# A perceiver kernel with two attention stages around 64 experts: a longer second chain in the first stage, a norm on another engine, and scores at another place in the second stage

## The chip, the cores and the metric

The kernel runs on one core of a Trainium2 chip. The metric is the device time of one execution, in microseconds (us); for the kernel before it is 2828.25 us, the median of three runs (2827.0 to 2829.42). A core has a matrix engine (TensorE, "PE" in the profile, with its weight loads as "PEld"), a vector engine (VectorE, "DVE"), an activation engine (ScalarE, "ACT"), a general engine (GpSimd, "POOL") and a queue of transfers that is fed by SyncE ("SP"). Each engine works through its own instructions in order, and the engines wait for each other by semaphores.

## The reference, cut to what matters

All data is float32. There are 64 sequences of 32 tokens, width 256 (2048 tokens in all), and 64 contexts of 257 rows of width 256, one for each sequence. Two layers follow each other; every step is added to the token stream x.

- Layer 0, cross attention: tokens are layer-normed twice, context rows once (with gain g and offset b); keys and values come from the context rows and the sequence's own tokens; 16 heads of 64; queries and keys are divided by their root mean square; softmax over 289 positions with a mask.
- Layer 0, self attention over the 32 tokens of a sequence, 16 heads of 16, with normed queries and keys.
- Layer 0, mixture of experts: a gate takes 8 of 64 experts for each token, an expert holding 128 tokens at most; every expert is a gated product 256 to 128 to 256. A shared gated product (512 wide) is added with a sigmoid gate.
- Layer 1, cross attention to the same contexts (257 rows), then a self attention with latent projections and a rotation of the positions, then a feed-forward of three 256x256 products in a row and a tanh.

The steps that the change touches most are, for a context of layer 0, the norm and the attention:

```
xn = (x - mean(x)) / sqrt(var(x) + eps) * g + b
k, v = split([xn, ln] @ Wkv)
attn = softmax(where(mask, rmsnorm(q) @ rmsnorm(k).T * scale, -max))
out = (attn @ v) @ Wout + bout
```

with mean and variance over a row's 256 values and ln the sequence's own normed tokens. All other steps are left as they are by the change.

## The kernel before, in words

The 2048 tokens are 16 tiles t of 128 tokens; tile t holds sequences s = 4t to 4t + 3, and b is the place of s in its tile. x stays on the chip for the whole run. PSUM, where products land, is cut into 8 banks (`bank`), which are given out in turn. TensorE's instructions run in the order in which the program is written; the other engines' orders come from a scheduler that follows modelled times. Most work is written as Python generators; each `yield` is a place where the other chain's work can be put in between.

**Stage 1** (`before`, L372). The first chain, of class CrossFirst, goes over the contexts s:
- `load` brings the context rows (cx, 2 x 128 x 256).
- `prepare` (L1156) norms them: statistics and two TENSOR_SCALAR on VectorE (`layernorm`, L140), then gain and offset by two instructions on GpSimd (L1160, L1161).
- `turn` transposes them (L1173) and copies them to xT (L1176, ScalarE; the sequence's own tokens by L1177).
- `keys` makes the keys in eight column blocks (32 matmul instructions of 289 columns, L167 psA<-xT,wk), copied to kT by L1201 and L1203 in turn, and squares them to `sq` (L1206).
- `norms` sums the squares over a head (L1218), `spread` spreads them over the rows (L1239), `scores` makes the scores (L1258) and the softmax (L1267, L182, L184, L197).
- `weigh` transposes the weights (L207) and copies them to `at` (L208); `values` multiplies `at` with cx (L221) and then with the value weights, with a copy to yT (L231, L233).

`queries(t)` (L1090) prepares a tile's queries: the two norms, transposes, the product with wq and more transposes. In the loop (L467) the pieces of several contexts are interleaved: keys, norms, spread and scores of s + 2, turn of s + 3, prepare of s + 4, load of s + 5, weigh and values of s. The second chain, `tail` (L516), takes a finished tile through the output product and the addition to x (`heads_out`, L237), the first self attention (`self_first`, L527: `normed`, product to qk, L552 transposes, L573 scores, softmax over heads, `attend_self` with the transposed weights eT of L297 and the products of L310), and the gate (`route`: L614, L617 and the writing of the tokens to their experts' rows, L645). It is resumed by `slot()`, each call of which takes every running chain one `yield` further. There are three slots for each s and two in the last s of a tile, so 11 for each tile; a tile's tail takes 14 resumptions, and tile 14's has an extra pause of HOLD resumptions.

**Stage 2** (`experts`, L656). Each of 64 experts has its weights fetched 12 ahead (AHEAD), its tokens transposed and three products. At expert 12 `after_weights` (L795) loads the weights of stage 3 and makes two derived weights on TensorE: the latent weights, and the feed-forward's three matrices joined to one (`ffn_weights`, from f_a, L167 psA<-f_a,f_a1T and psA<-mid,f_wT). The shared product's pieces are spread between the experts.

**Stage 3** (`after`, L808). For each s: scores of s + 2 (L167 psY<-xT,qk, softmax L1357 and L1358), a slot, `weigh` of s (transposes L1375, copies to `at` L1376), a slot, `values` of s (L167 psA<-at,cx, L1388). The chain in the slots is `follow`: output product, second self attention (`self_second`, with transposes L1003 and L1014, copy to qTl L1005), feed-forward. `combine` gathers the experts' rows of a tile (L780) and adds them to x (L791).

Two flags differ between the stages: `slack`, off in stage 1 and on in stage 3, adds one pause behind a norm and one in `attend_self`.

Of the kernel before, what the change touches and what calls it, by code (L numbers as in the profile page):

```python
# [14 lines left out]
ALU = mybir.AluOpType  # L15
# [69 lines left out]


def done(steps):
    for _ in steps:
        pass


class Kernel:
# [58 lines left out]

    def normed(self, t):

        z = self.wk.tile([P, 1, D], F32, name="z")
        self.layernorm(z, self.x[:, t : t + 1, :])
        yield
        if self.slack:
            yield
        zT = self.wk.tile([P, 2, P], F32, name="zT")
        self.transposed(zT, z[:, 0, :])  # L160
        yield
        return z, zT
# [5 lines left out]

    def add_to_x(self, t, ps, bias=None):
        nc, xt = self.nc, self.x[:, t, :]  # L170
        if bias is not None:
            nc.gpsimd.tensor_tensor(xt, xt, bias, ALU.add)
        nc.vector.tensor_tensor(xt, xt, ps, ALU.add)
# [62 lines left out]

    def heads_out(self, t, yT, wv, wo, bias, split=False):  # L237


        nc = self.nc  # L240
        oT = self.wkh.tile([P, 8, P], F32, name="oT", tag="q", bufs=1)
        for half in range(2):
            ps = self.bank("psY")
            for p in range(4):
                for odd in range(2):
                    h = 2 * (4 * half + p) + odd
                    at = h // 4 * 4 + PLACES[h // 4 % 2].index(h % 4) if split else h
                    self.product(
                        ps[DH * odd : DH * odd + DH, p * P : (p + 1) * P],
                        [wv[:, k, h * DH : (h + 1) * DH] for k in range(2)],  # L250
                        [yT[:, k, at, :] for k in range(2)],
                    )
            nc.any.tensor_copy(
                oT[:, 4 * half : 4 * half + 4, :].rearrange("p a b -> p (a b)"), ps
            )
        yield
        ps = self.bank("psY")
        self.product(ps[:, :D], [oT[:, p, :] for p in range(8)], [wo[:, p, :] for p in range(8)])
        self.add_to_x(t, ps[:, :D], bias)

# [29 lines left out]

    def attend_self(self, t, e, recip, wo, bias):

# [4 lines left out]
        nc.vector.transpose(eT.rearrange("p a b -> p (a b)"), e.rearrange("p a b -> p (a b)"))  # L297
        yield
        if self.slack:
            yield  # L300

# [70 lines left out]
    def before(self, ctx):  # L372


        self.eb, self.vb, self.slack = 1, 2, False
        tc, nc, a = self.tc, self.nc, self.a
# [42 lines left out]
        cross.prepare(0)  # L419
        next(first)  # L420
        next(first)
        cross.prepare(1)
        for i in range(2):
            cross.load(i + 2)
            cross.turn(i)
            cross.keys(i)
            cross.norms(i)
            done(first)
            cross.spread(i)
            cross.scores(i)  # L430
        cross.load(4)
        cross.prepare(2)
        cross.prepare(3)
        cross.turn(2)

# [80 lines left out]
    def tail(self, t, yT, wv, wo, bo, sw, swo, sg, gw):  # L516

        yield from self.heads_out(t, yT, wv, wo, bo, True)
        yield
        if t == self.nt - 2:  # L520

            for _ in range(HOLD):
                yield
        yield from self.self_first(t, sw, swo, sg)
        yield from self.route(t, gw)

    def self_first(self, t, sw, swo, sg):  # L527
        nc = self.nc
        _, zT = yield from self.normed(t)
        qk = self.wk.tile([P, 2 * H, HS], F32, name="qk1", bufs=1)  # L530
# [10 lines left out]
            qk[:, :H, :], qk[:, :H, :], sg.unsqueeze(1).to_broadcast([P, H, HS]), ALU.mult  # L541
        )
        ps = self.bank("psA")
        self.product(ps[:, :D], [zT[:, k, :] for k in range(2)], [sw[:, k, 2 * D :] for k in range(2)])
# [40 lines left out]
        yield  # L585
        yield from self.attend_self(t, e, recip, swo, None)

    def route(self, t, gw):
# [29 lines left out]
        nc.vector.tensor_scalar(pr, pr, tot, None, ALU.mult)  # L618

        yield  # L620

# [34 lines left out]
    def experts(self, ctx, slot, tails):  # L656
# [94 lines left out]
        for e in range(E):  # L751
            weigh(e + AHEAD)
            fetch(e + 3)
            turn(e + 2)
            while (at - total + rest) * E < rest * e:
                next(side)
                at += 1
            inner(e + 1)
            outer(e)
            if e == AHEAD:  # L760
                self.after_weights()
        done(side)

# [33 lines left out]
    def after_weights(self):  # L797
# [7 lines left out]
        self.lat = self.latent_weights(w)  # L805
        self.ffnw = self.ffn_weights(w)

    def after(self, ctx):  # L808
        self.eb = self.vb = 1
        self.slack = True  # L810
        nc, n = self.nc, self.nb
# [25 lines left out]
        for s in range(n):  # L837
            t, b = divmod(s, NB)
            if s + 3 < n:
                cross.load(s + 3)  # L840
            if s + 2 < n:
                cross.scores(s + 2)
            if b == NB - 2 and t + 2 < self.nt:
                steps.append(cross.queries(t + 2))
                if t + 3 < self.nt:
                    steps.append(self.combine(t + 3, 3))
            slot()
            cross.weigh(s)
            slot()
            if s < 2:  # L850

                slot()
                slot()
            cross.values(s)
            if b == NB - 1:
                steps.append(self.follow(t, cross.yT, wv, wo, bo))
            slot()
# [112 lines left out]
    def self_second(self, t, wl, bl, wvo, bvo, wqk, bqk, wo, bo):  # L970
        nc = self.nc
        _, zT = yield from self.normed(t)
        lat = self.wk.tile([P, 2 * H, LAT], F32, name="lat", bufs=1)
# [42 lines left out]
        nc.any.tensor_copy(kT, ps)  # L1016
        yield


# [23 lines left out]
        yield  # L1043
        yield from self.attend_self(t, e, recip, wo, bo)

# [17 lines left out]
    def ffn(self, t, m, bias):  # L1063
        nc = self.nc
        _, zT = yield from self.normed(t)
        ps = self.bank("psA")
# [12 lines left out]
class CrossFirst:  # L1079
# [11 lines left out]
    def queries(self, t):  # L1091
# [7 lines left out]
        nc.gpsimd.tensor_tensor(ln[:, 0, :], ln[:, 0, :], self.bl, ALU.add)  # L1099
        yield  # L1100
        lnT = k.wkx.tile([P, 2, P], F32, name="lnT")
        k.transposed(lnT, ln[:, 0, :])
# [6 lines left out]
        for n in range(2):  # L1109
# [9 lines left out]
                q[:, 8 * n : 8 * n + 8, :], v, self.gam.unsqueeze(1).to_broadcast([P, 8, DH]), ALU.mult  # L1119
            )  # L1120
        nc.vector.tensor_scalar(ss, ss, float(DH) * 1e-16, None, ALU.max)
        nc.scalar.activation(ss, ss, AF.Ln)
# [33 lines left out]
    def prepare(self, s):  # L1156

        k, nc, cx = self.k, self.k.nc, self.cx[s]
        k.layernorm(cx, cx)
        nc.gpsimd.tensor_tensor(cx, cx, self.gx.unsqueeze(1).to_broadcast([P, 2, D]), ALU.mult)  # L1160
        nc.gpsimd.tensor_tensor(cx, cx, self.bx.unsqueeze(1).to_broadcast([P, 2, D]), ALU.add)  # L1161

# [123 lines left out]
class CrossSecond:  # L1286
# [7 lines left out]
    def queries(self, t):  # L1294

        k, nc = self.k, self.k.nc
        _, zT = yield from k.normed(t)
        qT = k.wk.tile([P, 8, P], F32, name="qT", bufs=1)
# [173 lines left out]
```

## Time and profile before

| | |
|---|---|
| median of three runs | 2828.25 us |
| the profiled execution | 2804.67 us |
| its span, first to last instruction | 2802.8 us |
| mean granted TensorE clock | 0.982 of full |
| moved to and from memory | 157.03 MB, mean 56 GB/s |
| costliest TensorE group, keys product (L167 psA<-xT,wk) | 517.4 us busy, 2048 instructions |
| busiest ACT group, squares (L1206) | 149.4 us, 128 instructions |
| busiest DVE groups: copies to kT (L1203), score products (L1267) | 108.4 and 102.1 us |
| POOL's gathers (L780) and writings (L645) | 131.5 and 126.5 us |

The profile is of one execution. Its page gives the busy time of each engine, the same in 40 slices of the span, the costliest groups of instructions, and the chain of work that ended last. A group's line reads: code line, engine, operation, output<-inputs, sizes, count | busy us, mean ns of one | idle time of the engine just before, and what ended most of it. The list of waits sums such idle times by what the engine waited for. Stretches are given in us from the start of the span: stage 1 runs to about 1508, the last tile's second chain to 1570, stage 2 to about 1760, stage 3 from there to the end.

### The profile page before, as it was taken

To read this page: it belongs to the slowest core of one execution; us is meant where nothing else is said; L and a number is where in the kernel's file an instruction comes from. 1 tells how busy PE (TensorE), PEld (TensorE's weight loads), DVE (VectorE), ACT (ScalarE), POOL (GpSimd) and SP (SyncE) were. 2 spreads that over 40 slices of the span, in tenths; PEclk is the share of its full clock that TensorE was granted. 3 is DMA by queue.
4 is the path that set the end of the run, shared out by engine and by line. 5 is a ranking of instruction groups with operands and counts; after the bars stand their busy time and mean duration, and the time that the engine had idled before them with its cause. 6 is when DMAs were issued, how large, how long until landed. Compare 5 with 4: busy or idle time off the path is not lost. (4 is left out here: it accounts for less than half of the span.)

```text
span 2802.8 us, 58905 instructions
## 1 busy us (share of the span) xinstructions
PE 2657.6 (95%) x23386; PEld 1824.5 (65%) x23386; DVE 1694.9 (60%) x4427; ACT 1241.6 (44%) x3436; POOL 684.3 (24%) x756
## 2 busy tenths in 40 slices
PE   6999999999999999999999799999999999999996
PEld 3556666666666666666666578667777777777764
DVE  5546666666666666666665433466666666666664
ACT  3455555555555555555554223333333333333331
POOL 5211333133313331243121200321212222121001
PEclk8999999999999999999999899999999999999997
DMA  8000011011000000000001677321211222222110
GB/s 271 16 14 18 31 33 31 18 31 33 29 18 27 26 22 18 20 19 16 18 7 38 233 237 243 91 67 54 58 51 50 59 52 58 56 51 55 33 35 5
DMA packets 136087, 157.03 MB, mean 56 GB/s; under 512 B 24024, under 2 KB 118979, under 8 KB 135812
## 3 DMA queue, kind: packets, MB, share of 16 engines
q1 hardware_dynamic: 114308, 119.65, 13.8%
q0 software_dynamic: 12288, 25.21, 3.4%
q10 hardware_dynamic: 9216, 8.39, 0.9%
q8 instruction: 185, 3.03, 0.4%
q14 instruction: 90, 0.74, 0.1%
HBM read 121.63 MB, written 37.75 MB: 57 GB/s over the span
## 5 line engine op out<-in xcount | busy, mean ns | idle before, releaser
L167 PE MATMUL psA<-xT,wk 128*128 128x289 f32 x2048 | 517.4, 411 | 7.9 <-ACT xT L1176 4.5
L167 PEld LDWEIGHTS psA<-xT,wk 128*128 128x128 f32 x2048 | 388.0, 191 | 134.8 <-issue 21.8
L780 POOL DMA_INDIRECT y<-oute,idx x128 | 131.5, 1028 | 643.4 <-DVE x L791 453.9
L167 PE MATMUL psA<-at,cx 128*128 128x512 f32 x512 | 235.4, 602 | 20.0 <-ACT qTl L1005 18.2
L221 PE MATMUL psY<-at,cx 128*128 128x512 f32 x512 | 239.8, 612 | 0.1
L167 PE MATMUL psY<-xT,qk 128*128 128x257 f32 x1024 | 234.3, 382 | 0.0
L167 PEld LDWEIGHTS psY<-xT,qk 128*128 128x128 f32 x1024 | 190.8, 190 | 35.0 <-issue 10.2
L1357 DVE TENSOR_REDUCE mx<-psY 128x1 f32<-128x257 f32 x256 | 105.7, 423 | 133.6 <-PE psY L167 133.5
L1358 ACT ACTIVATE sim<-psY,mx 128x257 f32<-128x257 f32 x256 | 121.6, 476 | 142.3 <-DVE mx L1357 142.2
L184 ACT ACTIVATE sim<-sim,mx 128x289 f32<-128x289 f32 x256 | 134.1, 526 | 100.0 <-DVE mx L182 100.0
L221 PEld LDWEIGHTS psY<-at,cx 128*128 128x128 f32 x512 | 93.5, 192 | 123.0 <-issue 108.8
L167 PEld LDWEIGHTS psA<-at,cx 128*128 128x128 f32 x512 | 92.9, 190 | 120.8 <-issue 76.7
L233 ACT COPY yT<-psY 128x512 f32<-128x512 f32 x127 | 68.2, 589 | 220.7 <-PE psY L231 220.7
L645 POOL DMA_INDIRECT buf<-z,fi x128 | 126.5, 988 | 148.0 <-DVE fi L642 102.2
L1160 POOL TENSOR_TENSOR cx<-cx,a_gx 128x512 f32<-128x512 f32 x64 | 81.8, 1278 | 292.1 <-DVE cx L140 290.3
L1206 ACT ACTIVATE sq<-kT 128x1156 f32<-128x1156 f32 x128 | 149.4, 1167 | 4.4 <-DVE kT L1203 2.8
L1201 ACT COPY kT<-psA 128x289 f32<-128x289 f32 x256 | 94.8, 389 | 104.2 <-PE psA L167 104.2
L1376 ACT COPY at<-psT 128x512 f32<-128x512 f32 x145 | 78.8, 595 | 123.4 <-PE psT L1375 118.3
L1218 PE MATMUL psB<-sq,c 128*32 128x289 f32 x1024 | 109.4, 419 | 19.7 <-ACT sq L1206 19.5
L1388 DVE SCALAR_TENSOR_TENSOR yT<-at,xT,psA 128x512 f32<-128x512 f32 x128 | 94.0, 735 | 56.1 <-PE psA L167 50.7
L167 PE MATMUL psY<-yT,wv 128*64 128x128 f32 x2048 | 121.6, 275 | 1.6 <-DVE yT L1388 1.4
L1177 POOL COPY xT<-lnT 128x64 f32<-128x64 f32 x64 | 15.3, 240 | 423.0 <-PE psA L167 299.3
(257 smaller groups left out, 5190.5 us busy)
## 6 DMA issues: line engine op xcount, KB each, us to landing
cx<-in_ctx SPq DMA_DIRECT2D x128, 256.0 KB
we<-in_m_ew SPq DMA_DIRECT2D x64, 384.0 KB
xT<-in_ctxT SPq DMA_DIRECT2D x64, 257.0 KB
buf<-zero SPq DMA_DIRECT2D x32, 256.0 KB
be<-buf SPq DMA_DIRECT2D x64, 128.0 KB
oute<-oe ACTq DMA_DIRECT2D x64, 128.0 KB
mu<-in_mask SPq DMA_DIRECT2D x16, 128.5 KB
x<-in_x SPq DMA_DIRECT2D x16, 128.0 KB
```

The lines of the kernel that those rows point to most:

```text
L167: self.nc.tensor.matmul(ps, lhsT=lhs[i], rhs=rhs[i], start=(i == 0), stop=(i == n - 1))
L184: nc.scalar.activation(sim[:, g, :], sim[:, g, :], AF.Exp, bias=mx[:, g : g + 1], accum_out=sm[:, g : g + 1])
L221: nc.tensor.matmul(ps[kc], lhsT=values[i][:, kc * P : (kc + 1) * P], rhs=at[i], start=(i == 0), stop=(i == n - 1 and tail is None),)
L645: d = nc.gpsimd.indirect_dma_start(out=self.buf[:, :], out_offset=bass.IndirectOffsetOnAxis(ap=fi[:, k : k + 1], axis=0), in_=z[:, 0, :], ...
L780: nc.gpsimd.indirect_dma_start(out=y, out_offset=None, in_=self.oute[:, :], in_offset=bass.IndirectOffsetOnAxis(ap=self.idx[:, t, k : k + ...
L1160: nc.gpsimd.tensor_tensor(cx, cx, self.gx.unsqueeze(1).to_broadcast([P, 2, D]), ALU.mult)
L1201: nc.scalar.copy(kT[:, p, :], ps[:, :JK])
L1206: nc.scalar.activation(sq[p // 4], kT[:, p - 3 : p + 1, :], AF.Square)
L1218: nc.tensor.matmul(ps[g * 32 : (g + 1) * 32, :JK], lhsT=k.pair[odd], rhs=sq[p // 4][:, p % 4, :], start=(odd == 0), stop=(odd == 1),)
L1357: nc.vector.tensor_reduce(mx[:, g : g + 1], ps[:, :J], AX.X, ALU.max, negate=True)
L1358: nc.scalar.activation(sim[:, g, :], ps[:, :J], AF.Exp, bias=mx[:, g : g + 1], accum_out=sm[:, g : g + 1])
L1388: nc.vector.scalar_tensor_tensor(self.yT[:, c, :, b * S : (b + 1) * S], self.at[:, 2, :].rearrange("p (h i) -> p h i", h=H), xT[:, c, J - ...
```

## The change

- (a) The start of stage 1 is written in another order: four resumptions of the first queries ahead of the second context's norm; loads 2, 3 and 4 together; turn and keys of context 0, the rest of the first queries, turn of 1, norms of 0, prepare of 2, spread and scores of 0, keys of 1, turn of 2, norms of 1, prepare of 3, spread and scores of 1.
- (b) The tail of stage 1 takes 26 resumptions instead of 14: a pause behind the norm, qk apart from the values, nine pauses in `attend_self`, one more in `route`. `slack` becomes an argument that counts pauses. `queries` of CrossFirst has two more yields; its product with wq is made in two halves in different slots.
- (c) In stage 1 the output product is made in two halves of 128 columns, each with its own addition of bias (GpSimd) and product (VectorE) to x.
- (d) The HOLD pause of tile 14 in stage 1 is gone; in stage 3 it stays.
- (e) The contexts' norm has its gain and offset on VectorE: four SCALAR_TENSOR_TENSOR instead of two TENSOR_SCALAR on VectorE and two TENSOR_TENSOR on GpSimd.
- (f) `ffn_weights` is called at expert 24 instead of expert 12.
- (g) In stage 3 the scores of s + 2 come behind `weigh` of s instead of ahead of the slot in front of it.
- (h) `self_second` has one more yield ahead of its score product.

```diff
+def pause(n):
+    for _ in range(n):
+        yield
...
-    def normed(self, t):
+    def normed(self, t, steps=0):
...
-        if self.slack:
-            yield
+        yield from pause(steps)
...
-    def add_to_x(self, t, ps, bias=None):
-        nc, xt = self.nc, self.x[:, t, :]
+    def add_to_x(self, t, ps, bias=None, cols=slice(0, D)):
+        nc, xt = self.nc, self.x[:, t, cols]
...
-    def heads_out(self, t, yT, wv, wo, bias, split=False):
+    def heads_out(self, t, yT, wv, wo, bias, split=False, parts=1):
...
-        yield
-        ps = self.bank("psY")
-        self.product(ps[:, :D], [oT[:, p, :] for p in range(8)], [wo[:, p, :] for p in range(8)])
-        self.add_to_x(t, ps[:, :D], bias)
+        n = D // parts
+        for i in range(parts):
+            yield
+            cols = slice(i * n, (i + 1) * n)
+            ps = self.bank("psY")
+            self.product(ps[:, :n], [oT[:, p, :] for p in range(8)], [wo[:, p, cols] for p in range(8)])
+            self.add_to_x(t, ps[:, :n], bias[:, cols], cols)
...
-    def attend_self(self, t, e, recip, wo, bias):
+    def attend_self(self, t, e, recip, wo, bias, steps):
...
-        yield
-        if self.slack:
-            yield
+        yield from pause(steps)
...
-        next(first)
-        next(first)
+        for _ in range(4):
+            next(first)
         cross.prepare(1)
-        for i in range(2):
-            cross.load(i + 2)
-            cross.turn(i)
-            cross.keys(i)
-            cross.norms(i)
-            done(first)
-            cross.spread(i)
-            cross.scores(i)
-        cross.load(4)
+        for i in range(2, 5):
+            cross.load(i)
+        cross.turn(0)
+        cross.keys(0)
+        done(first)
+        cross.turn(1)
+        cross.norms(0)
         cross.prepare(2)
+        cross.spread(0)
+        cross.scores(0)
+        cross.keys(1)
+        cross.turn(2)
+        cross.norms(1)
         cross.prepare(3)
-        cross.turn(2)
+        cross.spread(1)
+        cross.scores(1)
...
     def tail(self, t, yT, wv, wo, bo, sw, swo, sg, gw):
-        yield from self.heads_out(t, yT, wv, wo, bo, True)
-        yield
-        if t == self.nt - 2:
-            for _ in range(HOLD):
-                yield
+        yield from self.heads_out(t, yT, wv, wo, bo, True, 2)
+        yield
...
-        yield from self.attend_self(t, e, recip, swo, None)
+        yield from self.attend_self(t, e, recip, swo, None, 9)
...
             if e == AHEAD:
                 self.after_weights()
+            if e == 2 * AHEAD:
+                self.ffnw = self.ffn_weights(self.w2)
...
-            if s + 2 < n:
-                cross.scores(s + 2)
             if b == NB - 2 and t + 2 < self.nt:
...
             slot()
             cross.weigh(s)
+            if s + 2 < n:
+                cross.scores(s + 2)
             slot()
...
-        yield from self.attend_self(t, e, recip, wo, bo)
+        yield from self.attend_self(t, e, recip, wo, bo, 2)
...
     def prepare(self, s):
         k, nc, cx = self.k, self.k.nc, self.cx[s]
-        k.layernorm(cx, cx)
-        nc.gpsimd.tensor_tensor(cx, cx, self.gx.unsqueeze(1).to_broadcast([P, 2, D]), ALU.mult)
-        nc.gpsimd.tensor_tensor(cx, cx, self.bx.unsqueeze(1).to_broadcast([P, 2, D]), ALU.add)
+        mv, rs = k.stats(cx, 2)
+        for j in range(2):
+            x = cx[:, j, :]
+            nc.vector.scalar_tensor_tensor(x, x, mv[:, j, 0:1], self.gx, ALU.subtract, ALU.mult)
+            nc.vector.scalar_tensor_tensor(x, x, rs[:, j : j + 1], self.bx, ALU.mult, ALU.add)
```

More of the change, by code (lines that the diff above doesn't have):

```diff
@@ L372, in before @@
     def before(self, ctx):
-        self.eb, self.vb, self.slack = 1, 2, False
+        self.eb, self.vb = 1, 2
         tc, nc, a = self.tc, self.nc, self.a
@@ L528, in self_first @@
         nc = self.nc
-        _, zT = yield from self.normed(t)
+        _, zT = yield from self.normed(t, 1)
         qk = self.wk.tile([P, 2 * H, HS], F32, name="qk1", bufs=1)
@@ L618, in route @@
         nc.vector.tensor_scalar(pr, pr, tot, None, ALU.mult)
+        yield
         yield
@@ L805, in after_weights @@
         self.lat = self.latent_weights(w)
-        self.ffnw = self.ffn_weights(w)
     def after(self, ctx):
         self.eb = self.vb = 1
-        self.slack = True
         nc, n = self.nc, self.nb
@@ L971, in self_second @@
         nc = self.nc
-        _, zT = yield from self.normed(t)
+        _, zT = yield from self.normed(t, 1)
         lat = self.wk.tile([P, 2 * H, LAT], F32, name="lat", bufs=1)
@@ L1017, in self_second @@
         yield
+        yield
         ps = [self.bank("psB") for _ in range(4)]
@@ L1064, in ffn @@
         nc = self.nc
-        _, zT = yield from self.normed(t)
+        _, zT = yield from self.normed(t, 1)
         ps = self.bank("psA")
@@ L1100, in queries @@
         yield
+        yield
         lnT = k.wkx.tile([P, 2, P], F32, name="lnT")
@@ L1120, in queries @@
             )
+            if n == 0:
+                yield
         nc.vector.tensor_scalar(ss, ss, float(DH) * 1e-16, None, ALU.max)
@@ L1296, in queries @@
         k, nc = self.k, self.k.nc
-        _, zT = yield from k.normed(t)
+        _, zT = yield from k.normed(t, 1)
         qT = k.wk.tile([P, 8, P], F32, name="qT", bufs=1)
```

## The prediction

> **What bounds the kernel.** The engine totals come first.
>
> ```profile
> PE 2657.6 (95%) x23386; PEld 1824.5 (65%) x23386; DVE 1694.9 (60%) x4427; ACT 1241.6 (44%) x3436; POOL 684.3 (24%) x756
> ```
>
> TensorE is idle for 2802.8 − 2657.6 = 145 us, and the change takes no matmul work away: 145 us, plus what a withdrawn clock costs, is all that order can win. The table by stretches says where it lies (columns: stretch, length, busy PE, PEld, DVE, ACT, POOL, granted clock, DMA share, GB/s).
>
> ```profile
> 0.00:130.00 130.00, 97.84 (x534) 57.53 (x538) 68.48 (x167) 54.54 (x148) 50.62 (x67) 0.92 0.45 152
> 130.00:1508.00 1378.00, 1345.71 (x11380) 860.82 (x11384) 871.47 (x2442) 750.00 (x2022) 399.46 (x461) 1.00 0.08 22
> 1508.00:1570.00 62.00, 43.45 (x610) 28.19 (x605) 33.95 (x115) 20.36 (x64) 10.34 (x13) 0.81 0.41 145
> 1570.00:1660.00 90.00, 81.84 (x404) 59.79 (x403) 26.91 (x80) 24.86 (x67) 7.80 (x8) 0.94 0.66 219
> ...
> 1760.00:1870.00 110.00, 103.05 (x654) 79.16 (x653) 58.58 (x143) 40.78 (x108) 39.55 (x40) 0.97 0.26 76
> 1870.00:2720.00 850.00, 829.36 (x8453) 618.73 (x8452) 556.36 (x1301) 304.62 (x896) 165.90 (x159) 1.00 0.19 52
> 2720.00:2803.00 83.00, 56.62 (x743) 37.41 (x741) 41.08 (x81) 15.50 (x43) 9.63 (x9) 0.79 0.02 6
> ```
>
> The idle time is 32 us in the start, 32 in the rest of stage 1, 19 at the border to stage 2, 8 early in stage 2, 7 at the start of stage 3, 21 in its steady part and 26 at the end. What TensorE waits for there (total, times, longest):
>
> ```profile
> PE psB L1218 <- ACT sq L1206: 19.5, 23, 2.1
> PE psA L167 <- ACT qTl L1005: 18.2, 12, 1.7
> ...
> PE psY L310 <- DVE at L208: 14.7, 14, 1.3
> PE psT L149 <- DVE z L140: 12.5, 6, 4.1
> PE psA L167 <- DMA f_a<-in_f_a: 4.8, 1, 4.8
> ```
>
> Three recur once a tile: L310 on `at` (14 times), L1218 on `sq` (17 times after 130 us), and the product on qTl (12 times). In the timeline (start, length, operation; idle time ahead in brackets):
>
> ```profile
> 64.26 10.20 PE L167 MATMUL psA<-xT,wk 128*128 128x289 f32 x32 [0.82 <-ACT xT L1176]
> 332.01 1.24 PE L310 MATMUL psY<-eT,vz 32*32 32x32 f32 x122 [1.04 <-DVE at L208]
> 1633.27 3.75 PE L167 MATMUL psA<-f_a,f_a1T 128*128 128x256 f32 x8 [4.80 <-DMA f_a<-in_f_a]
> 2009.64 3.67 PE L167 MATMUL psA<-at,cx 128*128 128x512 f32 x8 [1.75 <-ACT qTl L1005]
> ```
>
> **Part by part, gains positive.**
>
> *Start, 0 to about 157 us.* The new order sets another block of matmuls between a producer and its user: keys(0) | first queries | turn(1) | norms(0), and turn(2) between keys(1) and norms(1). From 23 us on, waits on `sq`, `xT`, `nk`, `rs` and issue sum to 9.3 + 4.5 + 1.7 + 0.7 + 3.4 = 19.6. Removed are the `xT` waits of 0.68 and 0.82 and most of the `sq` waits (0.58, 2.00); kept is norms → spread, adjacent as before (1.13 at 59 us), and contexts 2 and 3 get less lead. I count a fifth of the stalls, 4, and 4 of clock. [...] But keys products take 9.73 (27 us) and 10.20 (64 us) against 7.97 later, and L1218 2.14 against 1.17 behind an idle 2.00: 1.8 + 2.2 + 1.0 = 5 us of clock behind short gaps; with 4 of them, +8. The rows decide: **+8** (0 to +15).
>
> *Stage 1, the longer tail.* The waits from 130 us on are L310 14.7, L1218 12.3 − 2.1 that still belongs to the start, and 2.7 on yT (L573): 27.6, or 1.84 for each of 15 tiles. The tail's pieces now spread over 26 resumptions, 11 slots to a tile, so each slot behind `weigh` has something: z and heads' products (3.9 us), sel and a half of the query product (2.35), L573 (1.7), L310 with qk (1.7). In the built program, L310's fourth bank no longer reuses the bank that `at`'s copy frees; its 1.04 goes. What is late next is VectorE where context 3 of a tile meets the next tile's first: the head softmax (its rows sum to 3.7 us), a norm, two layer norms of queries and the context's norm give 22 us of VectorE under 23.6 us of TensorE. I estimate 1.2 us a tile from that closeness (0.3 to 3). Gain: 15 × (1.84 − 1.2) = **+9** (−17 to +23).
>
> *Output product in halves.* 16 matmuls of 128 columns instead of 8 of 256: by L167's rate, the same streaming; one more bank, and one more POOL add and VectorE add of 128x128 a tile. **−1** (−2 to 0).
>
> *Contexts' norm on VectorE.*
>
> ```profile
> L140 DVE TENSOR_SCALAR cx<-cx,mv,rs 128x256 f32<-128x256 f32 x128 | 61.8, 515 | 7.4 <-ACT rs L120 7.4
> L791 DVE SCALAR_TENSOR_TENSOR x<-y,w,x 128x256 f32<-128x256 f32 x128 | 59.8, 467 | 0.3
> L1160 POOL TENSOR_TENSOR cx<-cx,a_gx 128x512 f32<-128x512 f32 x64 | 81.8, 1278 | 292.1 <-DVE cx L140 290.3 <-DVE rs L118 1.0 <-issue 0.8
> ```
>
> Two L140 go (2 × 0.515), four SCALAR_TENSOR_TENSOR come (4 × 0.467 by L791, the same shape): +0.84 us of VectorE a context, 54 us over 64. [...] So 54 us; VectorE's share of the stage goes from 63 to 67%. TensorE's matmuls hide it, except in the context counted above; without that cover it is 54 us (the rival below). POOL loses 1.278 + 1.270 a context, which shortens the context's path to `turn`; that was not waited for in the steady part: 0.
>
> *Border, 1508 to 1570.* The last tail's chain runs 1525.8 to 1568.4 and is bound by latency; its own dependent steps stay. Dropping the pause and lengthening the tail lets tails 13 and 14 reach further past the loop, and their VectorE work meets the last tail's (5 us), while about 2 us of matmuls that fill leave the loop: **−3** (−10 to +5).
>
> *FFN weights at expert 24.* SP's issue of these loads hardly moves: they wait for the space of the latent weights in both orders. What moves is TensorE's product: it sat on the transfer for 4.80 and then ran at lowered clock ((3.75 − 1.89) + (2.86 − 1.89) = 2.8 for the two products): 7.6. Twelve experts later the data has long landed. Some may come back, as the stretch behind carries 237 to 243 GB/s: **+6** (0 to +7.6).
>
> *Stage 3, scores behind `weigh`.* qTl's copy follows L1003's transposes by L1375's 1.47 and then nothing; 1.5 us are missing, 12 times. Now the scores' product (16 matmuls of 257 columns at 0.23 each, 3.7 us) stands between `weigh`'s transposes and the product on `at`, and covers both copies. The softmax of those scores starts 2 us or so later but is needed two contexts on. **+17** (10 to 19). At the start of stage 3 the same scores no longer cover the wait for z of tile 1 (4.10 at 1800 us): **−3** (−6 to −1).
>
> *End.* One more step in the second attention, behind a chain bound by latency: **−1** (−3 to +1).
>
> Sum: 8 + 9 − 1 + 0 − 3 + 6 + 17 − 3 − 1 = **+32**. The profiled execution takes 2804.67, its span 2802.8, the median 2828.25, 23.6 above; the stalls are counted in the span, and I assume the same distance: 2804.7 − 32 = 2772.7 profiled, 2828.25 − 32 = **2796** as median.
>
> **Rivals.** (1) *Slower: the context's norm holds VectorE's queue in stage 1.* In the built order the four instructions stand among the score products and ahead of the next kT copies (L1217) on an in-order engine; kT releases `sq`, and `sq` L1218. For: L1218 waits for it 17 times already, and VectorE holds 22 of 23.6 us in one context of each tile. Against: in the other three it has 3 us or more of slack. If the whole 0.84 shows in each context, 54 us go, the other parts leave 32 − 9 = 23, and the time is 2828 − 23 + 54 = 2859. It decides from 23/64 = 0.36 us a context. (2) *The stage-3 gain comes back as another wait*: with scores late, `weigh` two contexts on waits for the softmax (0.9 for `sim` today), and in stage 1 the 1.84 stays at another line. Against: two contexts are 23 us. Then 17 and 9 become 5 and 0, the sum 11: 2817. With the start at nothing too, 2825, no change.
>
> **How the numbers follow.** Main case 0.70, around 2796; gain returned 0.15, of which half is within 0.2% of 2828.25 (5.7 us, about what a measurement of this kernel can tell from no change); slower 0.15. The good ends of all parts sum to some 70; I take six sevenths of it as the low bound, 2768. Upwards the range has to reach past case 2 and a little into case 1: 2836. Faster 0.70 + 0.06 = 0.76, same 0.09, slower 0.15.
>
> **What would show it.** Right: qTl's wait (18.2) and f_a's (4.8) are gone and nothing of that size is at L167 in stage 3; L310 no longer waits for `at`; the stretch to 1508 ends some 15 us earlier. Wrong: L1218 waiting on kT or `sq` more than 23 times, or `at` waiting for VectorE in every context; a border longer than 70 us; a scores-to-`weigh` wait in stage 3.

## The result, and the profile after

The changed kernel takes 2834.56 us (median of 17 runs, 2829.66 to 2840.46) against 2827.6 for the kernel before (17 runs beside it): a ratio of 1.0025, interval 1.0018 to 1.0032. It is slower, by 7 us; the prediction said 32 us faster. The profiled execution takes 2836.79, its span is 2834.7. The profile of before above (2804.67) is 24 us below the median of the kernel before: as the runs below show, this kernel takes 2804 on one occasion and 2821 to 2828 on others, so I compare profiles stretch by stretch, and say for each number from which occasion it is.

The totals of the page after, to be read against the first fence of the prediction:

```profile
PE 2667.6 (94%) x23642; PEld 1835.3 (65%) x23642; DVE 1728.6 (61%) x4559; ACT 1227.6 (43%) x3448; POOL 532.7 (19%) x644
```

TensorE is busy 10 us more (256 more matmuls, and slower ones), VectorE 34 us more, GpSimd 152 us less. The table by stretches, with the edges moved (columns as before):

```profile
130.00:1524.00 1394.00, 1350.39 (x11486) 866.12 (x11485) 903.72 (x2520) 734.01 (x2014) 261.22 (x353) 0.99 0.07 22
1524.00:1610.00 86.00, 62.88 (x747) 38.94 (x746) 39.64 (x169) 22.93 (x72) 25.93 (x29) 0.77 0.33 114
...
1890.00:2735.00 845.00, 821.40 (x8290) 614.76 (x8289) 541.73 (x1270) 301.45 (x890) 162.65 (x158) 1.00 0.20 52
2735.00:2835.00 100.00, 66.66 (x911) 45.23 (x909) 47.44 (x103) 20.32 (x60) 9.64 (x9) 0.82 0.02 5
```

Stage 1 idles 44 us in 1394, where it idled 32 in 1378, and has lost a little clock, 0.99 for 1.00. The row of the border is 86 us long where it was 62, but its edges stand at other places of the work: from the last context's values product to the first expert's transposes it takes 78.9 us against 67.3. Stage 3 idles 24 us where it idled 21, and the end 33 where it idled 26. TensorE's waits, summed over the span:

```profile
PE psA L172 <- ACT zT L156: 21.7, 34, 3.2
PE psT L155 <- DVE z L146: 20.4, 9, 6.4
PE psA L172 <- issue: 16.8, 34, 2.4
...
PE psB L1232 <- ACT sq L1220: 15.3, 19, 2.3
...
PE psY L316 <- issue: 8.4, 9, 2.2
PE psY L172 <- DVE yT L1402: 7.3, 15, 0.9
```

Three waits that the change aimed at are gone: `at` at the product of eT (14.7 us), qTl in stage 3 (18.2) and f_a (4.8). A fourth, that of L1218 (now L1232) for `sq`, went from 19.5 us only to 15.3. In their place stand waits of other names: zT, yT, and "issue", a wait for nothing that the profile shows. Here is one of the latter, in the tenth tile of stage 1 (all engines; left-out lines are other instructions):

```profile
944.92 1.20 PE L1272 MATMUL psB<-kT,qTf 64*32 64x289 f32 x31
...
947.74 0.27 PE L155 MATMUL psT<-c,z 128*128 128x128 f32 x1 [1.02 <-ACT ss L1135]
...
947.94 0.97 POOL L653 DMA_INDIRECT buf<-z,fi  x1 [0.30 <-issue]
948.47 0.27 PE L155 MATMUL psT<-c,z 128*128 128x128 f32 x1 [0.46 <-issue]
...
949.16 4.23 PE L172 MATMUL psA<-xT,wk 128*128 128x289 f32 x7 [0.42 <-issue]
...
950.70 1.56 DVE L1281 TENSOR_TENSOR sim<-psB,sim 128x289 f32<-128x289 f32 x4 [4.04 <-remote]
```

The scores (L1272) are over by 946.7, but VectorE, which multiplies them, gets TensorE's signal only at 950.7, 4 us late. Meanwhile single matmuls start 0.7 us apart, and the keys product runs seven matmuls in 4.23 us where it takes about 1.8 (in part because the granted clock falls to 0.50 from 949.0 us; see the last section). It begins while GpSimd issues the last of the eight scatters (L653) of a tile, and ends 1.8 us behind them. The same place of a run in which it does not happen (own_on_act, below):

```profile
922.11 1.20 PE L1272 MATMUL psB<-kT,qTf 64*32 64x289 f32 x32
...
923.25 0.44 PE L155 MATMUL psT<-c,z 128*128 128x128 f32 x2
923.52 2.85 PE L172 MATMUL psA<-xT,wk 128*128 128x289 f32 x11
923.75 1.55 DVE L1281 TENSOR_TENSOR sim<-psB,sim 128x289 f32<-128x289 f32 x4
```

VectorE starts 0.4 us after the scores end, though here too a scatter is being issued. I call the first case "silenced". The kept traces also record when each engine's signals come. In a silenced run TensorE's are missing from this record at all of a kernel's 15 or 16 sets of eight scatters but one or two, for stretches of up to 9 us; in the runs that I call not silenced hardly one is. It is not TensorE alone: in the changed kernel, up to 1500 us and from the start of such a set to 3 us behind its last scatter, 92 of 179 signals of TensorE are missing, 62 of 132 of ScalarE and 24 of 146 of VectorE; in the first profile of before none of 211, 212 and 282; in own_on_act 2 of 238, 12 of 190 and none of 246. A missing record is not yet a late signal; that signals come late is shown by who starts late, as VectorE above. Nor does the loading of instructions explain it: in the shown case no transfer of instructions starts between 934.1 and 952.1 us, and such transfers take as long in stage 1 of a silenced trace as in one that is not (medians of 1.0 to 1.2 us on one queue and 0.4 to 0.5 on the other).

### The profile page after: what moved, and what is told of

It is laid out like the page before. It is cut to its first block, busy times and chain, and to the rows that moved or that the text cites. A ratio compares the mean times of both kernels' runs of the same rounds, so it can differ in the third digit from the quotient of the medians.

```text
span 2834.7 us, 59398 instructions
## 1 busy us (share of the span) xinstructions
PE 2667.6 (94%) x23642; PEld 1835.3 (65%) x23642; DVE 1728.6 (61%) x4559; ACT 1227.6 (43%) x3448; POOL 532.7 (19%) x644
## 4 chain that ended last, share of the span: by engine, by line
PE 80%; DVE 8%; ACT 7%; issue 3%; DMA 1%; another core or an unknown queue 0%; POOL 0%; SPq 0%; POOLq 0%; ACTq 0%; DVEq 0%
PE psA L172 33%; PE psY L172 19%; PE psY L226 8%; PE psT L1389 3%; PE psB L1232 3%; PE psY L236 2%; PE psT L212 2%; PE psB L1272 2%; PE psY L316 2%; PE psB L172 1%; PE psA L1332 1%; PE psT L155 1%; ACT sim L189 1%; PE psR L1253 1%; ACT sim L1254 1%
## 5 line engine op out<-in xcount | busy, mean ns | idle before, releaser
L172 PE MATMUL psA<-xT,wk 128*128 128x289 f32 x2048 | 532.5, 416 | 18.2 <-issue 14.4
L1281 DVE TENSOR_TENSOR sim<-psB,sim 128x289 f32<-128x289 f32 x256 | 101.4, 449 | 78.4 <-PE psA L172 27.3
L653 POOL DMA_INDIRECT buf<-z,fi x128 | 126.5, 989 | 94.0 <-DVE fi L650 51.9
L1390 ACT COPY at<-psT 128x512 f32<-128x512 f32 x130 | 71.1, 586 | 133.4 <-PE psT L1389 69.9
L172 PEld LDWEIGHTS psY<-yT,wv 128*64 128x64 f32 x2048 | 115.0, 137 | 16.3 <-DVE yT L1402 11.2
L178 DVE TENSOR_TENSOR x<-x,psY 128x256 f32<-128x256 f32 (+1 forms) x80 | 29.2, 365 | 157.8 <-PE psY L172 156.2
L172 PE MATMUL psY<-wo,oT 128*128 128x128 f32 (+1 forms) x768 | 124.2, 315 | 0.0
```

The lines of the kernel that those rows point to most:

```text
L172: self.nc.tensor.matmul(ps, lhsT=lhs[i], rhs=rhs[i], start=(i == 0), stop=(i == n - 1))
L653: d = nc.gpsimd.indirect_dma_start(out=self.buf[:, :], out_offset=bass.IndirectOffsetOnAxis(ap=fi[:, k : k + 1], axis=0), in_=z[:, 0, :], ...
L1281: nc.vector.tensor_tensor(sim[:, g, :], ps[i][:, :JK], sim[:, g, :], ALU.mult)
```

## The experiments

Medians are set against the kernel before, taken on the same chip at the same time. It took 2803.6 in the first group of runs (1 to 4), 2824.1 in the second (5 to 8), 2827.5 in the third (9 to 12) and 2820.9 in the fourth (13 and 14). The first two groups were on the same chip, so it is not the chip that sets this. The traces of the first group are not silenced; those of the other three are wherever the kernel has its scatters. "Tiles" are the times from one tile to the next in the steady part of stage 1, if nothing else is said.

**1. own_on_act.** From the changed kernel:

```diff
-        nc.gpsimd.tensor_copy(xT[:, :, J - 1 : JK - 1], lnT[...])
-        nc.gpsimd.tensor_copy(xT[:, :, JK - 1 :], self.xlT[...])
+        nc.scalar.copy(xT[:, :, J - 1 : JK - 1], lnT[...])
+        nc.scalar.copy(xT[:, :, JK - 1 :], self.xlT[...])
```

> The changed kernel with one edit: the two small copies in turn that put a sequence's own tokens into xT run on ScalarE instead of GpSimd. Theory A (the scatter of route now stands on GpSimd's queue ahead of these copies, and the keys product waits for them): the stage-1 tiles from the fourth on, 94.3 to 96.6 us in the changed kernel's profile, come down to about 92, the issue stalls of 0.7 us an instruction vanish, and the median goes from 2834.6 to some 2806 (2800 to 2815). Theory B (the scatter's transfers themselves slow TensorE's issue): the stalls stay, 2834 give or take 4. Theory C (VectorE's load from the contexts' norm makes the tiles longer): no change either.

Measured: 2768.79, ratio 0.9878 (0.9863 to 0.9893), tiles of 90.4 us, below what any of the theories gave. It looks like theory A, but it was not: no_scores, in the same group, has these copies on GpSimd as the changed kernel has, and 90.4 too; and best1, in the second group, has them on ScalarE and tiles of 94. Theory A falls. What the run does show is the change without silencing: its TensorE instructions and their order are those of the changed kernel.

**2. scores_only.** The kernel before with `cross.scores(s + 2)` behind `cross.weigh(s)`, part (g).

> The kernel before with part (g) alone: in stage 3 the scores of s + 2 behind weigh of s. The prediction's step: 12 to 13 waits of 1.5 us go and nothing comes, minus 3 at the start of stage 3, so about 2814. Rival from the changed kernel's trace (the scores had covered two waits for zT and one for yT, which now show as 0.73, 0.46 and 0.46 us a tile): a tile of 61.97 instead of 61.54, 6 us over 14 tiles and 2 to 4 at the stage's start, so about 2836.

Measured: 2814.88, ratio 1.0042 (1.0028 to 1.0056), 11 us slower than the kernel before beside it: the loss that the rival forecast, but not by its waits. qTl's wait is gone, and in its place stands one of 1.21 us a tile for qf (1760 to 2810 us):

```profile
PE psB L1026 <- DVE qf L1011: 14.5, 12, 1.2
```

Most tiles of stage 3 take 61.4 us instead of 61.54, a gain of 0.16 each and not of 1.5. Two take 66.5 and 64.8 us, why was not tried; and the end is 3.8 us longer (61.7 us from the last values product of stage 3, against 57.9).

**3. norm_only.** The kernel before with part (e), the four SCALAR_TENSOR_TENSOR in `prepare`.

> The kernel before with part (e) alone: gain and offset of the contexts' norm on VectorE. If TensorE hides it, as the prediction has it: 2827.6 give or take 3, tiles of 93.5 us as before. If VectorE's queue is what holds stage 1 (rival 1 of the prediction): up to 0.84 us a context, 54 us, 2880; a quarter of it would already be 2841.

Measured: 2792.56, ratio 0.9965 (0.9951 to 0.9978): 10 us faster where the expectation had none, tiles of 93.2 instead of 93.5. Rival 1 is refuted. The instructions themselves are dearer than I had them (changed kernel):

```profile
L1175 DVE SCALAR_TENSOR_TENSOR cx<-cx,rs,a_bx 128x256 f32<-128x256 f32 x128 | 62.8, 514 | 2.4 <-ACT rs L126 0.5
L1174 DVE SCALAR_TENSOR_TENSOR cx<-cx,mv,a_gx 128x256 f32<-128x256 f32 x128 | 61.7, 483 | 0.0
```

2 × (0.514 + 0.483) − 2 × 0.515 = 0.96 us a context, 62 us in all, where the prediction had 54 from L791's row; hidden all the same.

**4. no_scores.** The changed kernel with the scores back ahead of the slot, so without (g) but with (h).

> The changed kernel without part (g): the scores of stage 3 are back ahead of the slot. By the prediction's step it loses 14: about 2849. By the rival (g costs 6 to 10): about 2826, with stage-3 tiles of 61.54 us again.

Measured: 2781.65, ratio 0.9921 (0.9907 to 0.9934). Its tiles in stage 1 are those of own_on_act, 90.4 us. Against own_on_act in the same group it is 13 us slower, all of it in stage 3 and the end: 63.2 us a tile there. So (g) is worth something where (h) is present, and costs 11 where it is not.

**5. before_again** and **6. after_again**: both kernels unchanged.

> The kernel before, unchanged, for a second profile and as a measure of the spread from chip to chip: its median was 2803.6 beside the first four experiments and 2827.6 beside the changed kernel. Ratio 1.000. Theory P (a chip of the slower sort slows TensorE's issue at certain places): where the median is near 2828, the profile shows stalls of 0.7 us an instruction that the first profile (2804.67) does not have; where it is near 2804, none.

> The changed kernel, unchanged. Its first stage is instruction for instruction that of no_scores on TensorE, VectorE and GpSimd, which ran at 90.4 us a tile; its third that of own_on_act. Theory P: on a chip where the kernel before takes about 2804, tiles of 90.4 and about 2770, ratio 0.988; on one where it takes about 2828, tiles of 94 to 97 and a ratio of 1.0025. Theory Q (the stalls belong to the program, and the GpSimd copies of own_on_act or the place of the scores in no_scores happened to remove them): tiles of 94 to 97 and a ratio of 1.0025 on any chip.

Measured: 2824.36 (1.0001) and 2825.15 (1.0005, 0.9996 to 1.0013). Both are silenced. The new profile of before shows what its first one did not:

```profile
1036.68 1.85 PE L1218 MATMUL psB<-sq,c 128*32 128x289 f32 x16
...
1041.28 0.98 POOL L645 DMA_INDIRECT buf<-z,fi  x1 [0.30 <-issue]
...
1043.60 0.46 DVE L1226 TENSOR_SCALAR nk<-psB 128x289 f32<-128x289 f32 x1 [4.75 <-PE psY L231]
...
1044.59 0.77 PE L1239 MATMUL psR<-nk,c 32*128 32x289 f32 x8 [1.37 <-ACT nk L1227]
```

The norms' sums (L1218) end at 1038.5; VectorE reads them at 1043.6, 5 us late, when the scatter is over. But TensorE has the long values products (L221, L231) in hand until 1043.2, and loses only 1.4 us.

**7. route_earlier.** The changed kernel with one `yield` less in `route`, ahead of the sel product.

> The changed kernel with one yield less in route, so that the scatter runs one slot earlier in the tile, under the keys and the values product instead of under scores, z and the first keys (the place that it had in the kernel before). If the stalls are tied to what TensorE issues at the scatter's end: on a slow chip tiles of about 91 to 92 instead of 94 to 97, some 35 us less than the changed kernel (2800); on a fast one no gain, 0 to 5 us more for sel coming too early. If they are not tied to it: as the changed kernel on either.

Measured: 2784.78, ratio 0.9864 (0.9849 to 0.9878), in a group where the changed kernel itself has 1.0005: this one yield is worth 40 us. The tiles take 91.4 us instead of 94.2. TensorE's signals still fail at 14 of 15 sets of scatters; they fail where little waits for them. The waits of after_again in stage 1 (400 to 1400 us):

```profile
PE psB L1232 <- ACT sq L1220: 13.1, 19, 0.9
PE psA L172 <- issue: 10.7, 29, 0.9
```

and those of route_earlier in the same stretch:

```profile
PE psB L1231 <- ACT sq L1219: 4.2, 11, 0.4
...
PE psB L1231 <- issue: 0.5, 1, 0.5
```

The issue wait of 10.7 us is nearly gone.

**8. best1.** The edits of own_on_act and no_scores together.

> The changed kernel with the own tokens' copies on ScalarE and without part (g). The first stage as own_on_act, 90.4 us a tile; the third as no_scores, 62.3 to 64 us a tile: about 2782 beside 2804 for the kernel before. If instead the longer stage-3 tiles of no_scores (63.96 in every second tile) were of that run alone, 61.54 a tile and about 2765.

Measured: 2834.45, ratio 1.0042 (1.003 to 1.0055): silenced, tiles of 94.3. A miss: the expectation took the first group for the rule.

**9. tail_only.** The kernel before with (b), (c), (d).

> The kernel before with the longer tail alone (parts b, c and d, with the queries' two added yields). The prediction gave these +9, -1 and -3 together. From the traces so far (stage 1 from the fourth tile on 1163.8 us before and 1117.4 in own_on_act, of which the norm alone brought 4.5; last values to first expert 67 before and 84 after): some -40 in stage 1 and +17 behind it, so about 2780 where the kernel before takes 2804, and about 2835 where it takes 2826, as the silent stretches of TensorE during the scatter then come on top.

Measured: 2840.55, ratio 1.0044 (1.0029 to 1.0059), silenced, tiles of 95 to 96.7: as expected for that case. Its working has two wrong terms, though: for own_on_act it took the values product of context 62 for the last one. To that of context 63, as for the kernel before, stage 1 from the fourth tile on takes 1126.1 us instead of 1117.4, and from there to the first expert 75.7 instead of 84.

**10. best2.** From the changed kernel: scores ahead of the slot, one yield ahead of the second attention's score product, one yield in route.

> The changed kernel without parts (g) and (h) and with the scatter a slot earlier. Stage 3 goes back to 61.54 us a tile and an end as before, 10 to 12 us less than route_earlier (2784.8): about 2774 where the kernel before takes 2824, about 2758 where it takes 2804. If (g) and (h) together are worth what the prediction gave (g), 17, it is slower than route_earlier by about that much.

Measured: 2776.8, ratio 0.9819 (0.9805 to 0.9832): 50 us faster than the kernel before beside it, though silenced, and below every median of the changed kernel. It differs from route_earlier by (g) and (h) alone; 0.9864 − 0.9819 = 0.45%, 13 us, is what the two cost together.

**11. no_scatter.** `for k in range(0)` instead of `range(TOPK)` around the scatter.

> The changed kernel without the eight indirect DMAs that write a tile's normed tokens to their experts' rows: the experts then work on zeros, with the same instructions. If it is the scatter that silences TensorE for 4 to 7 us, the silent stretches are gone and all tiles take 90.4 to 91 us: about 2772 on any chip. If something else of the longer tail does it (TensorE's instruction fetch, other queues), the tiles stay at 94 us where the kernel before takes 2824 or more, with about 2825.

Measured: 2771.9, ratio 0.9801 (0.9786 to 0.9816), in a group where best2, with its scatters, is silenced at 14 of 15 sets. No signal of TensorE is missing in stage 1, the tiles take 91.2 us, and no issue wait is left in stage 1 (400 to 1400 us):

```profile
PE psB L1232 <- ACT sq L1220: 5.2, 11, 0.7
PE psB L1272 <- ACT qTf L1152: 2.6, 10, 0.3
```

So it is the scatter that silences TensorE here.

**12. best3.** best2 with `9 if t < self.nt - 2 else 1` pauses.

> best2 with one pause instead of nine in the first self attention of the last two tiles. If the border's 17 us come of the length of the last tail, it wins 8 to 15 against best2: some 2762 where the kernel before takes 2824. If the border is held by the chain's own latency and not by the number of resumptions: as best2.

Measured: 2790.82, ratio 0.9872 (0.9857 to 0.9887), 14 us slower than best2 where a gain of 8 to 15 was expected: a miss. From the last context's values product to the first expert it takes 87.8 us instead of 78.8, and the waits there (1480 to 1580 us) name the reason:

```profile
PE psT L155 <- DVE z L146: 14.2, 4, 8.6
PE psT L559 <- POOL qk L546: 7.0, 1, 7.0
```

Tile 14's scatter now stands ahead of the last tile's qk on GpSimd's queue, and holds it for its 11.8 us: it ends at 1536.9 us, and qk starts there.

**13. before_no_scatter.** The edit of no_scatter on the kernel before.

> The kernel before without the eight indirect DMAs that write a tile's normed tokens to their experts' rows; the experts work on zeros with the same instructions. Theory: the kernel before takes 2804 on one occasion and 2824 to 2828 on others because of the stretches in which TensorE is silent during the scatter. Then without a scatter it takes about 2800 (2795 to 2805) also where it takes 2824 or more with one, ratio 0.991, and its tiles are 93.5 us throughout. If the occasions differ by something else, it stays within 8 us of the kernel before.

Measured: 2801.37, ratio 0.9932 (0.991 to 0.9954), tiles of 93.7. It is 19.5 us faster than the kernel before beside it, and within 3 us of what that takes in the first group with its scatters.

**14. h_only.** The kernel before with one more `yield` ahead of the second attention's score product.

> The kernel before with part (h) alone, the one more yield ahead of the score product in the second attention. The prediction gave it -1. From no_scores (which has h without g and 63.2 us a tile in stage 3 instead of 61.54, and an end of 68 us instead of 62): a loss of 15 to 25, so about 2846 where the kernel before takes 2826. If no_scores owed its longer tiles to something else, 2827 to 2830.

Measured: 2846.35, ratio 1.01 (1.0076 to 1.0124): 25 us slower for one yield. Its waits in stage 3 (1870 to 2720 us) against those of the changed kernel in the same stretch; first h_only:

```profile
PE psA L167 <- ACT sim L1359: 25.5, 13, 2.4
```

then the changed kernel, with (g) and (h):

```profile
PE psA L172 <- ACT zT L156: 15.2, 26, 0.7
PE psY L172 <- DVE yT L1402: 6.4, 13, 0.9
```

With (h) alone qTl's 18.2 becomes a wait of 25.5 for `sim`, and a tile of stage 3 takes 63.3 us; with both, 26 waits for zT and 13 for yT, and 61.97; with neither, 61.54.

## Why the prediction was wrong, step by step

The table sets the predicted gains beside those between landmarks of the traces (starts of the first values product, of the one of tile 3, of the last one, which is context 63's, of the first and last expert's transposes, of the first queries' product of stage 3, and so on): before against own_on_act (not silenced), and before_again against after_again (silenced). Gains are positive, in us. Five traces of kernels that have the old start and the old norm reach tile 3 at 353.0 to 357.4 us, so the first two rows are uncertain by some 4 us together.

| stretch | predicted | not silenced | silenced |
|---|---|---|---|
| start to first values | 8 (to 157 us) | 4.9 | 4.7 |
| to tile 3 | (in the next) | 5.3 | 3.6 |
| tile 3 to last values | 9 − 1 + 0 | 37.7 | −3.8 |
| border to first expert | −3 | −8.4 | −4.5 |
| experts | 6 | 6.8 | 9.1 |
| start of stage 3 | −3 | −0.5 | −1.0 |
| steady stage 3 | 17 | −7.4 | −5.6 |
| end | −1 | −2.6 | −7.3 |
| sum | 32 | 35.8 | −4.8 |

**What decided: a queue past which a step was moved.** The step of the prediction that failed is the working of the longer tail: it counted the tail's matmuls and VectorE's load, and put the eight scatters at the tail's end at nothing, without a reason. Twelve more resumptions carry them from under keys, norms and values to under the scores, z and the first keys. Unsilenced this costs nothing that shows: tiles of 90.4 us instead of 93.5. Silenced, stage 1 from tile 3 to the last values takes 1178.6 us (after_again) instead of 1126.1 (own_on_act; no_scores, whose stage 1 is the changed kernel's, takes 1126.8), 52.5 us; the kernel before pays 11 for the same silence (1174.8 against 1163.8), since there it falls on values products of 0.43 us a matmul. The difference, 41.5 us, is what turns a gain of 35.8 us in all (own_on_act) into a loss of 4.8 (after_again). No line of the first profile shows the silence, so its size could not be read; that the scatter would meet other work could. With it falls the assumption that the profile and the median stay 24 us apart: most of that distance was the silence, and the change made it larger.

**A right number would have been luck.** Without silence the gain is 35.8 us, close to the 32 forecast, but from other places: the tail gives some 30 us more than its share, stage 3 takes back 24 and the border 5. And that the 41.5 us of silence are near the prediction's error (2834.6 − 2796 = 39) is chance too: against the silenced kernel before, the tail and what goes with it miss their forecast by 12 us, stage 3 by 23 and the end by 6.

**The start**: +8, and the two first rows together gave 10.2 and 8.3, with some of the norm in it. The traces also settle what the start had of clock: from 25 to 157 us the granted clock was 0.5 for 23.9 us before and for 17.0 in own_on_act (17.1 and 13.6 in the silenced pair). If work takes at most twice its time at that clock, as the keys' matmuls do in the last section (0.48 us apart against 0.24), such a stretch costs at most half its length, and the new order won 3.5 and 1.8 us of clock, an estimate; the prediction's rows gave 4. The longest such stretch before, 13.7 us from 55.0, has no idle gap over 2.0 us in the 20 us ahead of it.

**The longer tail**, the scatter apart, has the right mechanism and too small a size: +9, where it brought most of 38 (the norm alone brings 4.5 there). I left 1.2 us a tile for VectorE's closeness; what is left is 0.26 (qTf, 3.1 us over 12 tiles). And I counted only the gaps ahead of L1218, 0.7 us a tile. The sixteen matmuls behind a gap also came drawn out, 1.85 us instead of 1.2 as the squares arrived piecemeal; by start-to-start times L1218 takes 7.16 us a tile before and 4.95 in own_on_act. A wait that hides inside a group's busy time was missed.

**The contexts' norm**: 0 predicted, a gain of 10 measured. VectorE's 62 us are hidden. Of the gain 4.5 us lie between tile 3 and the last values (1159.3 us against 1163.8), and the wait for `sq` names them: 3.5 us from 400 to 1400 us in norm_only, 7.7 before. Ahead of tile 3 it is 8 us against the first profile (349.3 against 357.4), but 4 against scores_only (353.0), whose start is the same as before's.

**The border**: −3 predicted (−10 to +5), −8.4 and −4.5 measured: the right way, and inside the range. Three tails instead of two reach past the loop, and the last one stands behind another's scatter on GpSimd: in own_on_act the last scatter ends 66.3 us after the last values, in the first profile 56.1.

**Stage 3**: here the second step failed, and it is wrong, not mis-sized: +17 predicted, −5.6 to −7.4 measured. The scores do cover qTl, and 18.2 us of waiting are gone. But the prediction asked what they would cover at the new place, and only at tile 1 what they had covered at the old one. With (g) alone qf comes out (1.21 us a tile) and a little of zT; with (g) and (h) zT twice and yT once a tile, 0.73 + 0.46 + 0.46 = 1.65 us against the 1.50 saved. The tile is 0.43 us longer, and the other 0.28 us stand in no wait. And (h), which got −1 at the end, costs 25 alone; the end loses 2.6 and 7.3 us.

**FFN weights** and **output halves** came out as predicted: f_a's wait is gone, its product takes 1.9 us instead of 3.75 (the granted clock was 0.50 from 1632.5 to 1638.0 us in the first profile of before, and is 1.00 at the product's new place, 1685 us), the experts' stretch is 7 to 9 us shorter; the halves add 0.22 us a tile (3.73 against 3.51).

Of the two rivals, 1 is refuted by norm_only. Rival 2, the gain coming back as another wait, is what happened in stage 3, with other names than the prediction gave; in stage 1 it came through a mechanism that I had not listed.

**Open.** Why TensorE is silenced in some groups of runs and not in others is not shown. The chip's number, the scatter's place in time and its length (about 1.0 us each) are the same. Nor is it shown by what path a scatter holds back the signals of TensorE, and with them those of ScalarE and VectorE.

## What to carry to other kernels

When a chain is stretched, list every instruction at its far end, its indirect transfers on GpSimd above all, and look at what the other engines do at the place where it now falls; here one `yield` there was worth 40 us. When work is moved to cover a wait, first name the waits that it covers where it stands. And where a profile's time is 24 us off the median of the runs, ask what the profile does not show: here some 20 of those 24 us were the scatter's (2801 us without it where it takes 2821 with it), and they decided the sign.

## What the runs showed of the hardware that I had not expected

- In the silenced runs, during eight indirect scatters of 128 rows of 1 KB (10 us in all), TensorE's signals came up to 5 us late and short matmuls started 0.7 us apart, though neither uses GpSimd. Without the scatters the kernel before takes 2801 instead of 2821 us, and the changed one 2772 where it is otherwise at 2825 or more. So a scatter slows TensorE here; the traces do not tell by what path.
- At some of the stalls the granted clock was lower as well. In the profile of the changed kernel the granted clock is 0.5 in six stretches of 3.4 or 6.8 us in stage 1, 23.9 us in all, each at a silenced scatter. The one in the case shown above (columns as in the table by stretches):

```profile
949.00:955.80 6.80, 6.55 (x13) 4.01 (x13) 4.55 (x7) 1.26 (x4) 4.15 (x5) 0.50 0.02 4
```

There the keys' matmuls start 0.48 us apart from 951.3 to 955.6 us, and 0.24 apart behind that. But after_again, silenced as well, has no such stretch from 130 to 1500 us. From tile 3 to the last values the first takes 1188.5 us and the second 1178.6, so the clock is the likely reason why the same kernel takes 2834.7 and 2824.7 us in its two profiles.
